# Two graph layers on one core: the second group's batches are measured together in the prologue, and its second batch takes its place among the first group's first layer

## The chip, the cores and the metric

The kernel runs on one core of one Trainium2 chip. The metric is the device time of one execution in microseconds (us); the time of record is the median of the runs shown. A profile is one further execution, taken by the hardware profiler. Engines are called as the profile calls them: PE (TensorE, matmul), PEld (its weight loads, which overlap PE), DVE (VectorE), ACT (ScalarE), POOL (GpSimd) and SP (SyncE, which issues all of this kernel's DMAs).

## The reference

The input x has 64 batches of 256 nodes with 512 features, all in float32, and one adjacency matrix of 256 by 256 serves all batches.

```python
# layer 0
h = relu(layernorm(x))
H = h @ W                                  # 512 -> 256
e = leaky_relu(H @ a[0] + (H @ a[1]).T, 0.2)
alpha = softmax(e where adj, else -1e9)
x = x + concat([alpha @ H, H])
# layer 1
h = relu(layernorm(x))
q, k, v = h @ Wq.T + bq, h @ Wk.T + bk, h @ Wv.T + bv     # 8 heads of 64
p = softmax(q k^T / 8 where adj, else -inf)
x = x + (p v) @ Wo.T + bo
```

## The kernel before, in words

**Tiling.** The 64 batches are taken in 32 groups of two. A batch is two tiles of 128 nodes (partitions) by 512 features. A group goes through first_norm (statistics, norm, a transpose into the operand hT0), first_layer (products ph with w0, attention of layer 0 with products po, then statistics, norm and transpose into hT1 for layer 1), project (q, k, v), scores, weigh and outputs. Products of layer 1 are made in seven block products instead of eight (Strassen's scheme in Winograd's form), whose operands need sums of the blocks: weight_sums and operand_sums. In the first two groups layer 0 uses plain products, four rows of ph and four of po.

**Norm and transpose.** stats gives bn_stats and bn_aggr on VectorE, factors gives minus the mean times the reciprocal deviation and that reciprocal (VectorE, then POOL), and norm gives xn on ACT, with two buffers. The first group's xn are turned on PE (pt). All others go the long way: VectorE transposes squares of 32 (xt, one buffer), SP sends them to DRAM (passed) and fetches them back in another order (moved, four DMAs), and put copies them on ACT into hT0 or hT1.

**What bounds the values.** judge checks that no score can overflow. It squares the weights on ACT, sums the squares on VectorE into `part`, and one small product on PE, `total`, adds them over the partitions. It is cut into pieces, which the driver takes through `next(verdict)`.

**The order.** Each engine works off its own queue in the order in which the program wrote it. not_sooner and after tie an instruction to the one before it on its engine, and in_order does so for every product on PE. The steps of the different groups are generators, and the driver at the end of `bounded` writes out by hand which of them takes its next step when:

- `norms` yields the pieces of first_norm of all groups, one after the other. For the second group before: measure and factors of batch 0; norm; turn and fetch; put into hT0; then the same four for batch 1.
- `pieces` yields the pieces of first_layer(1): one ph row each; with the fourth the row of scores (score_rows: a transpose on VectorE, the DMAs "line" and "own"); e and its exponential; its mask; four rows of po with their statistics, where the third also writes norm(0) and the fourth turn(0); norm(1); turn(1); put(0); put(1) with the operand sums.
- `products` yields the products of project(0), 7 each for q, k and v; `verdict` the pieces of judge; `bias` those of last_bias (bv_rows on VectorE, pb on PE); `edges` those of mask.
- late_loads issues the loads of wo_sb, bv_col, b_out and the third group's inputs on SP.

The loop over first_layer(0) (line 1068 of before) gives pieces to the numbered places of the first group's first layer. The list `order` (line 1094) then gives, for each product from the third on, first the letters n (a piece of norms) and s (a piece of first_layer(1)), and after them a piece of the verdict. After these comes the steady loop over the groups (`steps`), which the change does not touch.

Of the kernel before, what the change touches and what calls it, by code (L numbers as in the profile page):

```python
# [8 lines left out]
F32 = mybir.dt.float32  # L9
# [5 lines left out]
P = 128  # L15
# [26 lines left out]
def two_gnn_layers(tc, *args):  # L42

    nc = tc.nc
    with tc.tile_pool(name="verdict", bufs=1) as pool:
        wrong = pool.tile([1, 1], I32, name="wrong")
        bounded(tc, *args, wrong)  # L50
        again = nc.values_load(wrong[0:1, 0:1], min_val=0, max_val=1)
        with tc.If(again > 0):
            tc.strict_bb_all_engine_barrier()
            any_inputs(tc, *args)
# [3 lines left out]
def bounded(  # L58
# [27 lines left out]
    B, N, D = x.shape  # L86
    F1 = w0.shape[1]
    DH = 64
    HP = D // P
    NT = N // P  # L90
    GB = 2
# [9 lines left out]
    big = ctx.enter_context(tc.tile_pool(name="big", bufs=2))  # L101
# [81 lines left out]
    def mask():  # L183
        edge = att.tile([P, NT, N], F32, tag="kept", name="edge", bufs=3)
        not_sooner(vector, "tensor_scalar", edge, adj_i, 0.0, None, op0=ALU.not_equal)
        yield
        pt = mm("pt_mask").rearrange("p (k q) -> p k q", k=NT)
        for kb in range(NT):
            for t in range(NT):
                transpose(  # L190
                    pt[:, kb, t * P : (t + 1) * P], edge[:, t, kb * P : (kb + 1) * P], ident
                )
        not_sooner(vector, "tensor_copy", maskT, pt)

        not_sooner(vector, "reduce_max", bad[:, 0, :], edge, axis=AX.X)
        vector.tensor_scalar(bad[:, 0, :], bad[:, 0, :], 0.0, None, op0=ALU.is_equal)
        vector.tensor_tensor(edge, edge, adj_i, op=ALU.not_equal)
        vector.reduce_max(bad[:, 1, :], edge, axis=AX.X)
        yield
# [29 lines left out]
    def late_loads():  # L229
        rows = woT.rearrange("(q j h d) o -> j h d q o", j=QH, h=2, d=S)  # L230
        bv_rows = bv.rearrange("(q j h d) -> j h d q", j=QH, h=2, d=S)
        for j in range(QH):
            for half in range(2):
                not_sooner(
                    sync, "dma_start", w_sb["o"][j * S : (j + 1) * S, half, :4, :], rows[j, half]
                )
        for j in range(QH):
            for half in range(2):
                not_sooner(
                    sync, "dma_start", bv_col[j * S : (j + 1) * S, half, :], bv_rows[j, half]  # L240
                )
        not_sooner(
            sync, "dma_start", b_out,
            bass.AP(tensor=bo.tensor, offset=bo.offset, ap=[[0, P], [1, D]]),
        )
        load(2, 0)
        load(2, 1)
# [8 lines left out]
    def weight_sums(name, engine=vector):  # L256
        w = w_sb[name]
        not_sooner(engine, "tensor_sub", w[:, :, T3, :], w[:, :, W22, :], w[:, :, W12, :])
        engine.tensor_sub(w[:, :, T1, :], w[:, :, W12, :], w[:, :, W11, :])
        engine.tensor_sub(w[:, :, T2, :], w[:, :, W22, :], w[:, :, T1, :])  # L260
        engine.tensor_sub(w[:, :, T4, :], w[:, :, W21, :], w[:, :, T2, :])
# [11 lines left out]
    def last_bias():  # L273


        rows = att.tile([P, 2, D // 2], F32, tag="kept", name="bv_rows", bufs=3)
        for q in range(NQ):
            for half in range(2):
                of, by = w_sb["o"][:, half, 2 * q : 2 * q + 2, :], bv_col[:, half, q : q + 1]
                if q == half == 0:  # L280
                    not_sooner(vector, "tensor_scalar", rows, of, by, None, op0=ALU.mult)
                else:
                    vector.scalar_tensor_tensor(rows, of, by, rows, op0=ALU.mult, op1=ALU.add)
        yield
        pb = mm("pb")
        matmul(pb, square_ones, rows.rearrange("p o n -> p (o n)"), start=True, stop=True)
        yield
        not_sooner(vector, "tensor_add", b_out, pb, b_out)
        yield
# [126 lines left out]
    def stats(mv, src, t, name):  # L416
        st = small.tile([P, 6], F32, tag="st", name=f"st{name}_{t}", bufs=4)
        if vector.last:
            not_sooner(vector, "bn_stats", st, src[t])
        else:  # L420
            vector.bn_stats(st, src[t])
        vector.bn_aggr(mv[:, t, :], st)
# [87 lines left out]
    def operand_sums(engine, quads, sums):  # L510
        a11, a12, a21, a22 = quads
        s1, s2, s4 = sums
        not_sooner(engine, "tensor_add", s1, a21, a22)
        engine.tensor_sub(s2, s1, a11)

        not_sooner(engine, "tensor_sub", a21, a11, a21)
        engine.tensor_sub(s4, a12, s2)

    def seven(quads, sums):

        a11, a12, s3, a22 = quads
        s1, s2, s4 = sums
        return {
            1: (a11, W11), 2: (a12, W21), 3: (s4, W22), 4: (a22, T4),
            5: (s1, T1), 6: (s2, T2), 7: (s3, T3),
        }
# [3 lines left out]
    hT0 = {}  # L533

    def first_norm(g):

        xt = {}
        mv = small.tile([P, GT, 2], F32, tag="mv", name=f"mv0_{g}", bufs=4)
        factors, norm, turn, fetch, put = norm_T(xt, mv, f"0_{g}", g == 0)
        for b in range(GB):  # L540
            for t in range(NT):
                xt[b * NT + t] = xs[g, b][:, t, :]
                stats(mv, xt, b * NT + t, f"0_{g}")
            factors(b)
            yield
            norm(b)
            yield
            turn(b)
            if g == 1:
                fetch(b)  # L550
            yield
            if g <= 1:

                hT0[g, b] = big.tile([P, HP, N], F32, tag="hT0", name=f"hT0_{g}_{b}")
                put(b, hT0[g, b])
                if g == 1:
                    yield
        if g <= 1:
            return
        for b in range(GB):  # L560
            fetch(b, b == 1 or g == 2)
        yield
        for b in range(GB):
            hT0[g, b] = big.tile([P, HP, N], F32, tag="hT0", name=f"hT0_{g}_{b}")
            put(b, hT0[g, b])
            if b == 0:
                yield
        quads = [hT0[g, b][:, 2 * c : 2 * c + 2, :] for b in range(GB) for c in range(2)]
        sums = [
            att.tile([P, 2, N], F32, tag=tag, name=f"sums0_{g}_{tag}", bufs=bufs)  # L570
            for tag, bufs in (("r", 1), ("xn", 2), ("xn", 2))
        ]
        operand_sums(gpsimd, quads, sums)
        operands["first", g] = {i: form[0] for i, form in seven(quads, sums).items()}
        yield
# [202 lines left out]
    turn = [0]  # L778
# [279 lines left out]

    verdict = judge()
    norms = (piece for g in range(NG) for piece in first_norm(g))  # L1060
    bias, edges = last_bias(), mask()
    for piece in range(5):
# [4 lines left out]
    products, pieces = project(0), first_layer(1) if NG > 1 else iter(())  # L1067
    for piece, _ in enumerate(first_layer(0)):
        if piece == 1:
            next(norms)  # L1070
            next(norms)
            next(edges)
        elif piece == 2:
            next(norms)
        elif piece == 3:
            next(norms)
            late_loads()
        elif piece == 4 or piece == 9:
            next(verdict)
        elif piece == 10:  # L1080
            next(verdict)
            next(verdict)
            next(norms)
            next(norms)
            weight_sums("q")
        elif piece == 11:
            next(products)
            next(products)
    next(pieces)
    next(pieces)  # L1090
    next(norms)
    next(verdict)
    next(verdict)
    order = "n - - - - - nss n n ns sn ss ss s sn sn - s -".split()
    for i, parts in enumerate(order, 2):
        next(products)
        if i == 7:
# [18 lines left out]
    for g in range(NG):  # L1116
        products = project(g + 1) if g + 1 < NG else iter(())
        pieces = first_layer(g + 2) if g + 2 < NG else iter(())
# [419 lines left out]
```

## Time and profile before

| | |
|---|---|
| median of 3 runs | 2402.36 us (2402.26 to 2403.22) |
| profiled execution: its own time, its span | 2403.71 us, 2402.1 us |
| granted PE clock over the span | 0.999 |
| PE busy | 2379.1 us, 99% of the span |
| DVE, POOL, ACT busy | 1691.1, 1415.8, 1021.9 us |
| PE busy, 0 to 20 us | 10.85 us of 20 |
| PE busy, 60 to 120 us | 53.99 us of 60 |
| PE busy, 140 to 2300 us | all |

A line of a timeline reads: start, busy us, engine, line, operation, output <- input, shape, how often; in square brackets how long the engine stood before it and what released it. Nearly all lines say L35 or L137, which are those of helpers that record an instruction, so one goes by the names of the tiles. A matmul in float32 shows as two records. PEclk is the granted clock of PE as a share of full speed. A line of windows reads: the window, its length, then the busy time (and number of instructions) of PE, PEld, DVE, ACT and POOL, then PEclk, the DMA share and GB/s.

### The profile page before, as it was taken

The page shows a single profiled execution, that of the slowest core. Times are in us where ns is not written, and L with a number is a line of the kernel's source. Part 1 is how long each engine was busy: PE and PEld are TensorE (multiplying, and loading weights), DVE is VectorE, ACT ScalarE, POOL GpSimd, SP SyncE. Part 2 cuts the span into 40 slices and gives each one's busy share as a digit, 9 for nine tenths or more (in the row PEclk, how much of TensorE's full clock was granted, in tenths as well). Part 3 has the DMA queues.
Part 4 walks back from the last instruction along what each step waited for, and adds up shares of the span by engine and source line. Part 5 has one row for each costly group of instructions (what it writes and reads, how often), then busy time and mean ns, then how long its engine had stood idle before and what let it go on. Part 6 is the DMA issues. An engine that isn't in the chain of part 4 may idle for free.

```text
span 2402.1 us, 42948 instructions
## 1 busy us (share of the span) xinstructions
PE 2379.1 (99%) x15772; PEld 2005.1 (83%) x15772; DVE 1691.1 (70%) x3338; ACT 1021.9 (43%) x2017; POOL 1415.8 (59%) x1282
## 2 busy tenths in 40 slices
PE   8899999999999999999999999999999999999998
PEld 7788888888888888888888888888888888888886
DVE  7586766776766767667767677676677676676655
ACT  5543444444443434444444434344444444343431
POOL 3566556655556555666555575655665555656552
PEclk9999999999999999999999999999999999999999
DMA  6344445544454444455444555444554445444331
GB/s 197 101 137 156 134 146 154 158 145 142 136 157 149 153 151 134 144 155 157 145 141 136 159 150 159 142 136 145 154 158 146 142 136 158 150 150 152 109 105 46
DMA packets 272041, 343.76 MB, mean 143 GB/s; under 512 B 25424, under 2 KB 217168, under 8 KB 271824
## 3 DMA queue, kind: packets, MB, share of 16 engines
q1 hardware_dynamic: 271824, 340.95, 45.9%
q8 instruction: 126, 2.06, 0.4%
q14 instruction: 91, 0.75, 0.1%
HBM read 177.22 MB, written 163.64 MB: 142 GB/s over the span
## 4 chain that ended last, share of the span: by engine, by line
PE 96%; DVE 2%; DMA 1%; ACT 1%; SPq 0%; issue 0%; POOL 0%; ACTq 0%; DVEq 0%; POOLq 0%
PE pv L137 16%; PE py L137 16%; PE pk L137 16%; PE pq L137 16%; PE sc L137 10%; PE pr L137 9%; PE ph L137 8%; PE po L137 4%; DMA w_sb<-in_L_gnn_W_dram 0%; SPq L35 0%; DMA x<-in_x_dram 0%; DMA wo_sb<-in_L_gnn_Wo_dram 0%; ACT hT L35 0%; PE total L137 0%; DVE wk_sb L35 0%
## 5 line engine op out<-in xcount | busy, mean ns | idle before, releaser
L35 POOL TENSOR_TENSOR p<-p 128x512 f32<-128x512 f32 x248 | 378.7, 1539 | 491.7 <-DVE p L35 479.4
L35 ACT ACTIVATE xn<-x,factor 128x512 f32<-128x512 f32 x256 | 194.4, 807 | 329.6 <-POOL factor L35 327.7
L35 DVE TENSOR_TENSOR p<-p,maskT 128x1024 f32<-128x1024 f32 x254 | 327.6, 1309 | 3.1 <-ACT p L35 3.1
L35 DVE TENSOR_TENSOR x<-py,x 128x256 f32<-128x256 f32 x448 | 185.9, 415 | 187.4 <-PE py L137 181.0
L35 ACT ACTIVATE p<-sc 128x512 f32<-128x512 f32 x512 | 257.8, 624 | 140.9 <-PE sc L137 124.2
L35 POOL TENSOR_TENSOR parts<-parts 128x512 f32<-128x512 f32 x248 | 248.5, 1002 | 85.3 <-DMA parts<-rows 60.5
L137 PE MATMUL py<-wo_sb,oT 128*128 128x256 f32 x1024 | 262.4, 379 | 0.6 <-DVE oT L35 0.6
L137 PE MATMUL sc<-q,k 64*128 64x256 f32 x2048 | 252.3, 390 | 0.6 <-DVE oT L35 0.6
L137 PEld LDWEIGHTS sc<-q,k 64*128 64x128 f32 x2048 | 205.1, 186 | 48.4 <-issue 25.9
L137 PE MATMUL pk<-hT,wk_sb 128*128 128x256 f32 x1024 | 244.8, 382 | 0.0
L137 PE MATMUL pq<-hT,wq_sb 128*128 128x256 f32 x1024 | 240.0, 382 | 0.7 <-ACT hT L35 0.4
L137 PE MATMUL pv<-wv_sb,hT 128*128 128x256 f32 x1024 | 237.1, 379 | 0.0
L137 PE MATMUL pr<-p,v 128*32 128x256 f32 x4096 | 234.2, 380 | 0.0
L137 PEld LDWEIGHTS pq<-hT,wq_sb 128*128 128x128 f32 x1024 | 191.8, 190 | 36.2 <-issue 9.9
L137 PEld LDWEIGHTS pk<-hT,wk_sb 128*128 128x128 f32 x1024 | 189.7, 190 | 33.8 <-issue 10.4
L137 PEld LDWEIGHTS py<-wo_sb,oT 128*128 128x128 f32 x1024 | 194.2, 190 | 28.2 <-DVE oT L35 1.1
L137 PEld LDWEIGHTS pv<-wv_sb,hT 128*128 128x128 f32 x1024 | 194.4, 190 | 26.5 <-ACT kept_v L35 0.2
L35 POOL TENSOR_TENSOR factor<-factor,rexp 128x2 f32<-128x2 f32 x128 | 120.3, 940 | 162.9 <-DVE factor L35 162.7
L137 PEld LDWEIGHTS pr<-p,v 128*32 128x32 f32 x4096 | 126.8, 110 | 97.8 <-issue 17.6
L137 PE MATMUL py<-wo_sb,o_sums 128*128 128x256 f32 x768 | 197.6, 380 | 0.5 <-DVE x L35 0.5
L137 PE MATMUL pq<-sums,wq_sb 128*128 128x256 f32 x768 | 183.0, 381 | 3.4 <-ACT kept_q L35 3.4
L137 PE MATMUL pk<-sums,wk_sb 128*128 128x256 f32 x768 | 181.6, 379 | 0.5 <-ACT kept_k L35 0.5
(148 smaller groups left out, 4059.1 us busy)
## 6 DMA issues: line engine op xcount, KB each, us to landing
passed<-xt SPq DMA_DIRECT2D x124, 512.0 KB, 3.1
moved<-passed SPq DMA_DIRECT2D x496, 128.0 KB, 3.5
rows<-p SPq DMA_DIRECT2D x124, 512.0 KB, 3.4
parts<-rows SPq DMA_DIRECT2D x496, 128.0 KB, 3.0
x<-in_x_dram SPq DMA_DIRECT2D x64, 512.0 KB, 4.4
out_dram<-x SPq DMA_DIRECT2D x62, 512.0 KB, 3.9
own<-line SPq DMA_DIRECT2D x31, 256.0 KB, 3.1
wq_sb<-in_L_gnn_Wq_dram SPq DMA_DIRECT2D x2, 512.0 KB, 8.9
```

The costliest lines, as they stand in the source:

```text
L35: instruction = getattr(self.engine, operation)(*args, **kwargs)
L137: in_order(nc.tensor.matmul(*args, **kwargs))
```

## The change

For the second group, first_norm now measures both batches first, then norms, turns and fetches each in turn, and then copies both into hT0. For the other groups only the wording changes. The driver takes these pieces at other places: batch 1's measuring comes before the mask's second step, its norm and turn within the first group's first layer, and late_loads two pieces later. The second group's ph rows 0 and 1 are taken at piece 9, ahead of the first group's norm of layer 1 being turned on PE; rows 2 and 3 and the score row come ahead of the second piece of q's products that follow. In `order` the second group's attention (s) comes four to five products sooner, and the third group's norms (n) later.

```diff
@@ first_norm(g)
-        for b in range(GB):
+
+        def measure(b):
             for t in range(NT):
                 xt[b * NT + t] = xs[g, b][:, t, :]
                 stats(mv, xt, b * NT + t, f"0_{g}")
             factors(b)
+
+        def to_operand(b):
+            hT0[g, b] = big.tile([P, HP, N], F32, tag="hT0", name=f"hT0_{g}_{b}")
+            put(b, hT0[g, b])
+
+        if g == 1:
+            for b in range(GB):
+                measure(b)
+                yield
+            for b in range(GB):
+                norm(b)
+                yield
+                turn(b)
+                fetch(b)
+                yield
+            for b in range(GB):
+                to_operand(b)
+                yield
+            return
+        for b in range(GB):
+            measure(b)
             yield
             norm(b)
             yield
             turn(b)
-            if g == 1:
-                fetch(b)
-            yield
-            if g <= 1:
-
-                hT0[g, b] = big.tile([P, HP, N], F32, tag="hT0", name=f"hT0_{g}_{b}")
-                put(b, hT0[g, b])
-                if g == 1:
-                    yield
-        if g <= 1:
+            yield
+            if g == 0:
+                to_operand(b)
+        if g == 0:
             return
...
@@ driver
     for piece, _ in enumerate(first_layer(0)):
         if piece == 1:
+            for _ in range(3):
+                next(norms)
+            next(edges)
+        elif piece == 2 or piece == 3:
             next(norms)
+        elif piece == 4:
+            next(verdict)
             next(norms)
-            next(edges)
-        elif piece == 2:
-            next(norms)
-        elif piece == 3:
+        elif piece == 5:
             next(norms)
             late_loads()
-        elif piece == 4 or piece == 9:
+        elif piece == 8:
+            next(norms)
+        elif piece == 9:
             next(verdict)
+            next(pieces)
+            next(pieces)
         elif piece == 10:
             next(verdict)
             next(verdict)
-            next(norms)
-            next(norms)
             weight_sums("q")
         elif piece == 11:
             next(products)
             next(products)
+            next(norms)
     next(pieces)
     next(pieces)
-    next(norms)
     next(verdict)
     next(verdict)
-    order = "n - - - - - nss n n ns sn ss ss s sn sn - s -".split()
+    order = "- - - s - s - ss ss s sn n n n n sn - s -".split()
```

More of the change, by code (lines that the diff above doesn't have):

```diff
@@ L563, in first_norm @@
         for b in range(GB):
-            hT0[g, b] = big.tile([P, HP, N], F32, tag="hT0", name=f"hT0_{g}_{b}")
-            put(b, hT0[g, b])
+            to_operand(b)
             if b == 0:
```

## The prediction, made before the changed kernel ran

> **What bounds the kernel now.** I read the page's busy shares first, then busy time by window, then TensorE's waits, then the timeline of 20 to 135 us, where the change lies.
>
> ```profile
> PE 2379.1 (99%) x15772; PEld 2005.1 (83%) x15772; DVE 1691.1 (70%) x3338; ACT 1021.9 (43%) x2017; POOL 1415.8 (59%) x1282
> ```
>
> TensorE is the bound: 23 us of the span are not matmul. By windows, 9.2 us of that lie before 20 us (the first input), 6.6 us after 2300 us (the last output), and nothing from 140 to 2300. So the change can move only the stalls between 20 and about 135 us, and whatever TensorE loses or regains there shifts all the rest. Those stalls, by the view of waits (TensorE, 20 to 135 us: line, releaser, total, times, longest):
>
> ```profile
> PE pq L137 <- ACT kept_q L35: 3.8, 2, 3.4
> PE po L137 <- DVE e L35: 1.3, 1, 1.3
> PE sc L137 <- DVE oT L35: 0.6, 1, 0.6
> PE pk L137 <- ACT kept_k L35: 0.5, 1, 0.5
> PE pq L137 <- ACT hT L35: 0.4, 1, 0.4
> PE ph L137 <- ACT hT L35: 0.3, 1, 0.3
> ```
>
> One matters: the wait for kept_q. In the timeline of TensorE, and in two windows (busy us, then PEclk):
>
> ```profile
> 94.40 3.72 PE L137 MATMUL pq<-hT,wq_sb 128*128 128x256 f32 x16 [0.38 <-ACT hT L35]
> 101.57 3.46 PE L137 MATMUL pq<-sums,wq_sb 128*128 128x256 f32 x8 [3.45 <-ACT kept_q L35]
> 104.86 1.89 PE L137 MATMUL pq<-hT,wq_sb 128*128 128x256 f32 x8
> ...
> 108.82 1.99 PE L137 MATMUL pq<-hT,wq_sb 128*128 128x256 f32 x8 [0.34 <-ACT kept_q L35]
> ```
>
> ```profile
> 101.60:104.60 3.00, 3.00 (x7) 2.47 (x8) 3.00 (x3) 0.00 (x0) 3.00 (x2) 0.50 0.50 120
> ```
>
> TensorE stands 3.45 us, and the next product then takes 3.46 us where its like takes 1.89, at clock 0.50. The stall costs 5.0 us. The scalar queue makes it: kept_q is behind the copy of the second batch's hT, which waits 3.25 us for "moved". All stalls of 55 to 110 us together (0.3, 0.5, 1.3, 0.4, 5.0, 0.3) are 7.9 us: the most the change can win.
>
> **What the Trainium skill says.** "TensorE: Matmul & The Clock Gate", Part 1, lets the clock fall to half after an idle window of about 3.4 us; the row above agrees (3.45 us idle, then 0.50), while the 1.3 us wait left a 2.00 us product. I go by the trace: 1.57 us extra per stall over 3.4 us. "SBUF — State Buffer", section "SBUF: two separate sides", makes the port pair of VectorE and GpSimd an exclusive lock where a VectorE operation reads two SBUF inputs. The trace agrees (same operation, GpSimd first idle, then adding sums), and I price by these rows:
>
> ```profile
> 37.10 2.87 DVE L35 TENSOR_TENSOR wq_sb<-wq_sb 128x512 f32<-128x512 f32 x4
> 40.89 5.82 DVE L35 TENSOR_TENSOR wk_sb<-wk_sb 128x512 f32<-128x512 f32 x4
> ```
>
> **The change part by part**, from the built order of each queue. No work is added or removed; it is moved.
>
> (1) Batch 1's statistics go ahead of maskT. Four statistics and two factors, 2.0 us of VectorE, fall where it stood 2.08 us for pt_mask. The input was issued at about 6.3 us with 9.6 to landing, so it is there at 16. Cost 0. If that cover were gone, VectorE's 0.87 us ahead of e still hides part. On POOL its two factor operations (0.9 us) slip between residual adds whose reader, po's statistics, comes 8 us later: 0.
>
> (2) Batch 1's norm (ScalarE 26.0 to 27.5, idle before) and its two turns move ahead of the first group's second-layer statistics. On VectorE the turns take 27.3 to 28.6, so the reciprocal of po moves from 27.42 to 28.65, and with it the chain to xn.
>
> ```profile
> 32.44 1.52 ACT L35 ACTIVATE xn<-x,factor 128x512 f32<-128x512 f32 x2 [6.51 <-POOL factor L35]
> 33.40 1.27 PE L140 MATMUL pt<-ident,xn 128*128 128x128 f32 x8
> ```
>
> xn moves to 33.7 to 35.2. TensorE now wants ph of the second group's batch 0 straight after gram_k, at 33.4, and the scalar queue has that hT copy behind these two xn. Copy 35.2, first product 35.86 (0.66 after the copy's start, as at 57.80 to 58.46). **New stall S1: 2.46 us**, shorter than the clock's window, so no slow clock.
>
> (3) SyncE: passed (28.7) and four moved (31.3 to 33.1, landed by 36.5) precede wo_sb, bv_col, b_out and the third group's inputs, which slip 5.5 us. Their first users (bv_rows at 61, these statistics after 86) cover it. The row's transfer then goes line 50.8, two input loads, own 52.8; landing is 3.1 us alone, some 4.5 behind the loads: 57.3. Needed by VectorE at 59.4.
>
> (4) TensorE, start to start from before's rows: ph 3.49, pt 0.88, squares 1.79, pq 3.45, pt 0.88, ph 3.49, squares 1.78, from 35.86 to 51.6. Then five pq at 1.73; the fourth ends at 58.7. All inputs are in time: copies of hT1 at 46.4 to 47.5, POOL's sums 47.6 to 53.9. The row's transpose waits on VectorE for H (50.5), and wk_sb's sums stand behind it: at the 5.82 us of before they end at 56.6, ahead of q's sums.
>
> (5) From there VectorE is the queue that is late. After q's last sum (59.45) stand, in order: leaky e 1.49; bv_rows 0.48, 0.73, 1.41, 1.57 (before's steps, with POOL adding wo_sb between, as before); e by maskT 2.8 (0.68 each alone, about 1.65 and 1.15 against POOL's weight sums); k 0.7; wv_sb 4.24 as before; seven small sums 1.2. Sum 14.6: the first po reciprocal at 74. Two waits in between, kept_k for pk (about 1.1 us) and squares on ScalarE, stand inside this time.
>
> (6) Then the second group's second-layer statistics: three rows 1.62 apart plus 0.24 for factors, the fourth to bn_stats 1.5, a k sum 0.69, aggregate and factors 0.4: 7.6, so factor at 81.6. Now the queue order bites. ScalarE has xn of batch 1 (the "s" that calls norm(1)) **ahead of the four squares of w0**, and TensorE's "total" waits for the last sum of those squares, ahead of every pv. Before, the squares were at 73.08 and the norms came after total (75.82). Now: POOL 1.0, xn 1.56, squares 2.12, sum and semaphores 0.35: total at 86.6. TensorE, with pk and po done, is ready at 77.9. **New stall S2: 8.7 us** (part of it earlier, as pk's last product waits for that k sum). The clock falls in the first part, and one product runs before total, so I add 0.8 (0 to 1.6). What is queued behind total: seven pv 12.1 us, then scores.
>
> (7) Scores start at 86.6 + 0.25 + 12.1 + 0.8 = 99.75, against 90.10: 9.65 late. Everything feeding hT1 of group 1 is then early: its second moved lands near 95.5, the copy runs beside the scores, the kept_q stall is gone.
>
> (8) What is late next: the third group's hT copies stand ahead of the next kept_q on ScalarE. Their "moved" cannot leave before passed of its batch 1, which VectorE's turns send 5.9 us after the scores' start (95.98 before), as now. Passed and eight moved are 1.5 MB; landing was 15.1 us after the scores, about 14 without the other transfers; plus copies 1.15 and kept_q 0.9, the fourth pq starts 15.7 us after the scores, not 18.72. Of the 5.0 + 0.34 us only 3.0 come back (1.7 to 5).
>
> Sum: +9.65 - 3.0 = **+6.7 us**. Bounds: S1 2.0 to 3.0; VectorE's chain 14.6 is 10 if no port waits, 16.5 if all; later gain as said: -1 to +12. On the profiled execution (span 2402.1, own time 2403.7) that is span 2408.8, time 2410.4; on the median shown, 2402.36, it is 2409.0. About 0.2% (4.8 us) is what a measurement here can tell from no change.
>
> **Rivals.**
>
> *The port lock does not bite and VectorE keeps up (not slower).* Its place is queue step (5): where the first po reciprocal comes at 68.5 or sooner rather than 74, factor is set by po's last row from TensorE (72.7 + 3.5), total is at 81.2, scores at 93.6, 3.5 late, and 3.5 to 5 come back: -1.5 to 0, some 2401.5. For it: uncontended rows sum to 10. Against: before's bv_rows show 1.38 and 1.65 with POOL in the same place. Chance 0.24, with milder contention.
>
> *Both gifts fail (slower still).* S2 starts fully cold (1.6), own lands after 58.5, and the third group's copies stop TensorE over 3.4 us and cool it again (1.57): +11, 2413.4. Chance 0.12.
>
> *The change does what it says and no more: all stalls gone.* Then -7.9 us, 2394.5. It needs total not to wait for squares that stand behind xn; the built order excludes that unless VectorE is 8 us ahead of its rows. Chance 0.05.
>
> The likeliest, S1 and S2 with a partial return, has 0.59 and its own range 2406 to 2411.5. Slower by over 0.2% takes it and the second rival: 0.71; within 0.2% 0.24; faster 0.05. The range runs from the first rival to beyond the second: 2402 to 2414.
>
> **What would show it.** Right: TensorE waits for hT by ACT before ph at about 33.5 (2 to 2.5 us); a wait before total of several us, with PEclk near 0.5 around it, squares after four xn on ScalarE; no kept_q wait of 3.45 after the scores, but one of some 3 us ahead of the fourth pq. Wrong: total within 2 us of the last pk, VectorE idle between 60 and 80, or squares ahead of xn.

## The result, and the profile after

The changed kernel takes 2409.16 us (median of 10 runs, 2408.36 to 2410.52) against 2402.56 us for the kernel before in the same measurement (10 runs, 2402.26 to 2404.18). The ratio is 1.0026 with a 95% interval of 1.0017 to 1.0036: 6.6 us slower. The profiled execution has a span of 2408.1 us, against 2402.1.

First the page's busy times of the kernel after:

```profile
PE 2381.3 (99%) x15772; PEld 2007.2 (83%) x15772; DVE 1683.0 (70%) x3338; ACT 1021.2 (42%) x2017; POOL 1416.0 (59%) x1282
```

The numbers of instructions are the same. TensorE's busy time is 2.2 us longer, which is slow clock; the rest of the 6 us of span is standing. TensorE's waits after, 20 to 145 us (line, releaser, total, times, longest):

```profile
PE pk L137 <- DVE k L35: 3.6, 1, 3.6
PE pq L137 <- ACT kept_q L35: 3.5, 1, 3.5
PE ph L137 <- ACT hT L35: 1.4, 1, 1.4
PE total L137 <- DVE part L35: 1.4, 1, 1.4
```

Three waits that the kernel before did not have, and a wait for kept_q of the old size. The timeline of TensorE shows where each lies:

```profile
30.72 3.73 PE L137 MATMUL gram_k<-wk_sb 128*128 128x128 f32 x32
35.90 3.75 PE L137 MATMUL ph<-w_sb,hT 128*128 128x258 f32 x16 [1.45 <-ACT hT L35]
...
79.53 3.78 PE L137 MATMUL pk<-sums,wk_sb 128*128 128x256 f32 x8 [3.62 <-DVE k L35]
84.73 0.57 PE L137 MATMUL total<-part,square_ones 128*128 128x10 f32 x2 [1.42 <-DVE part L35]
85.14 5.24 PE L137 MATMUL pv<-wv_sb,hT 128*128 128x256 f32 x16
...
98.95 3.92 PE L137 MATMUL sc<-q,k 64*128 64x256 f32 x32
...
106.36 1.89 PE L137 MATMUL pq<-sums,wq_sb 128*128 128x256 f32 x8
...
115.22 3.46 PE L137 MATMUL pq<-hT,wq_sb 128*128 128x256 f32 x8 [3.52 <-ACT kept_q L35]
```

The product at 106.36 is the one that stood 3.45 us before the change; it stands no more. The one at 115.22, which stood 0.34, now stands 3.52 and runs at half clock.

One caution on reading two executions side by side. gram_k starts at 30.72 here and at 29.83 before, because the first layer's weights landed about 1 us later in this execution (VectorE waits 3.12 us for them after, 1.91 before); over the ten profiles of this study and the two of before and after that start ranges from 28.57 to 30.97 us, and the instructions ahead of the landing are the same. So I count from the start of gram_k to a later instruction of the same timeline, and take two marks: the first scores, and the first product for k behind the second batch's scores (134.66 before, 141.61 after). From that mark on TensorE is busy in both up to the tail, and what follows it takes 2266.3 to 2267.4 us in all twelve profiles.

| from gram_k's start, us | first scores | pr (p v) | second mark |
|---|---|---|---|
| before | 60.27 | 95.82 | 104.83 |
| after | 68.23 | 103.02 | 110.89 |

At the second mark the change has cost 6.06 us; the medians say 6.6. The loss to the first scores can be added up from the rows: 1.61 at ph (5.18 us behind gram_k instead of 3.57), 3.62 at pk and 1.89 because that product takes 3.78 and not 1.89, 1.42 at total, and 1.52 in the first pv (5.24 for what takes 3.72 at full clock): 10.06. The three stalls of before in this stretch (0.3, 0.5, 1.3) are gone: 10.06 - 2.1 = 7.96, which is 68.23 - 60.27. Then 1.90 us come back by the second mark.

The windows of the kernel after (length, busy time of PE, PEld, DVE, ACT and POOL, PEclk, DMA share, GB/s) show the clock low for ten microseconds, from 78.04 to 88.28:

```profile
74.63:78.04 3.41, 1.28 (x6) 0.78 (x5) 3.03 (x10) 1.10 (x2) 0.90 (x2) 1.00 0.00 0
78.04:81.46 3.42, 1.93 (x5) 1.57 (x6) 3.28 (x9) 1.03 (x2) 0.90 (x2) 0.50 0.00 0
81.46:84.87 3.41, 1.99 (x6) 1.12 (x5) 0.60 (x3) 3.32 (x12) 0.00 (x0) 0.50 0.40 158
84.87:88.28 3.41, 3.41 (x10) 2.78 (x11) 3.31 (x10) 0.25 (x1) 1.17 (x1) 0.50 0.83 271
```

And the timeline of ScalarE shows both queue orders that the forecast named:

```profile
80.85 1.52 ACT L35 ACTIVATE xn<-x,factor 128x512 f32<-128x512 f32 x2 [2.39 <-POOL factor L35]
82.28 0.40 ACT L35 ACTIVATE squares<-w_sb 128x256 f32<-128x256 f32 x1
...
111.51 1.14 ACT L35 COPY hT<-moved 128x512 f32<-128x512 f32 x2 [2.33 <-DMA moved<-passed]
113.29 1.14 ACT L35 COPY hT<-moved 128x512 f32<-128x512 f32 x2 [0.64 <-DMA moved<-passed]
114.34 0.83 ACT L35 ACTIVATE kept_q<-pq,bq_sb 128x256 f32<-128x256 f32 x2
```

The squares that total needs start only when the second batch's xn are through, and kept_q only when both copies of the third group's hT are. The larger wait, the one at pk, lies on VectorE, where the k sum stands behind the statistics of po's last row (VectorE's timeline of the kernel after):

```profile
78.80 0.67 DVE L35 TENSOR_TENSOR k<-pk,kept_k 128x512 f32<-128x512 f32 x1
```

### The profile page after: what moved, and what is told of

The parts are those of the page before. It is cut to its first block, busy times and chain, and to the rows that moved or that the text cites. A ratio compares the mean times of both kernels' runs of the same rounds, so it can differ in the third digit from the quotient of the medians.

```text
span 2408.1 us, 42959 instructions
## 1 busy us (share of the span) xinstructions
PE 2381.3 (99%) x15772; PEld 2007.2 (83%) x15772; DVE 1683.0 (70%) x3338; ACT 1021.2 (42%) x2017; POOL 1416.0 (59%) x1282
## 4 chain that ended last, share of the span: by engine, by line
PE 97%; DVE 2%; ACT 1%; DMA 0%; issue 0%; SPq 0%; POOL 0%; DVEq 0%; ACTq 0%
PE py L137 16%; PE pv L137 16%; PE pq L137 16%; PE pk L137 16%; PE sc L137 10%; PE pr L137 9%; PE ph L137 8%; PE po L137 4%; ACT xn L35 0%; DVE e L35 0%; DVE x L35 0%; DVE st L35 0%; PE pt L140 0%; DVE p L35 0%; PE total L137 0%
## 5 line engine op out<-in xcount | busy, mean ns | idle before, releaser
L35 DVE TENSOR_TENSOR p<-p,maskT 128x1024 f32<-128x1024 f32 x254 | 322.3, 1289 | 3.1 <-ACT p L35 3.1
```

The source lines that it names most:

```text
L35: instruction = getattr(self.engine, operation)(*args, **kwargs)
```

## The experiments

Ten kernels, each timed in five rounds. All but e9 start from the kernel after. The kernel before ran beside each of them, with medians of 2403.33 to 2403.60 us (2402.56 beside the kernel after), so kernels are compared by their ratios. A median carries the spread of the start told above, so the marks of the profile stand beside it.

| kernel | median us (runs) | ratio to before, 95% | first scores | second mark |
|---|---|---|---|---|
| e1_copy_first | 2407.15 (18) | 1.0018, 1.0011 to 1.0025 | 65.14 | 107.73 |
| e2_squares_first | 2409.27 (14) | 1.0024, 1.0016 to 1.0032 | 66.10 | 111.02 |
| e5_pool_later | 2406.86 (21) | 1.0016, 1.0009 to 1.0022 | 64.85 | 108.06 |
| e6_ksum_first | 2409.22 (13) | 1.0024, 1.0015 to 1.0032 | 66.92 | 111.62 |
| e4_kept_first | 2413.02 (5) | 1.0038, 1.0024 to 1.0052 | 68.54 | 113.93 |
| e9_before_kept | 2410.44 (6) | 1.0032, 1.0020 to 1.0045 | 60.39 | 112.75 |
| e7_copy_pool_squares | 2402.97 (13) | 1.0000, 0.9991 to 1.0008 | 59.13 | 103.61 |
| e8_all_four | 2405.05 (13) | 1.0007, 0.9999 to 1.0015 | 58.96 | 105.88 |
| e10_fetch_first | 2400.76 (13) | 0.9994, 0.9985 to 1.0002 | 58.94 | 103.52 |
| e12_fetch_one_put | 2404.14 (13) | 1.0004, 0.9996 to 1.0012 | 58.94 | 106.14 |

### e1: the hT copy ahead of the second batch's norm

```diff
-        elif piece == 8:
+        elif piece == 7:
             next(norms)
```

> The second group's first copy into hT0 stands ahead of the first group's two xn on ScalarE (in the changed kernel it stands behind them). Theory (queue order on ScalarE makes the stall ahead of ph): ph follows gram_k after 3.6 us instead of 5.2 and the gain runs on to the end, since VectorE's chain starts from q's fourth product: 1.3 to 1.6 us off, about 2407.7. Rival (what comes after is set by the row's transfer or by VectorE, not by q's products): the stall goes, but k's last product and total start when they did: within 0.4 us of the changed kernel.

ph follows gram_k in 3.57 us with no wait; the stall named S1 is this order on ScalarE. The second mark is 3.16 us sooner, the median 2.0 us lower (the intervals of the two ratios overlap, so it is the trace that decides). That is more than the 1.61 us of S1. The rest is clock; in the windows of this kernel it is back at 80.22 us:

```profile
76.80:80.22 3.42, 3.32 (x8) 2.52 (x8) 2.16 (x7) 1.96 (x5) 0.90 (x2) 0.50 0.28 114
80.22:83.63 3.41, 1.81 (x10) 1.42 (x9) 1.82 (x4) 2.22 (x8) 0.00 (x0) 1.00 0.43 140
```

The waits around it are as in the kernel after (3.62 and 1.60), and so is the 3.61 us product between them. Why the clock is back behind that product here, and only at 88.28 us in the kernel after, the twelve profiles show together. Between 20 and 148 us they hold 19 stretches of low clock, and these last 3.41 us (eleven), 6.83 (six) or 10.24 (two). In each of the seven profiles that have two of them, their starts lie a whole number of 3.41 us apart (78.04 and 115.58 in the kernel after: 11 times). So the clock changed only on a fixed grid of 3.41 us. Cut along this grid, the full clock fell after every step in which TensorE was busy for 1.33 us or less, and after none with 1.82 us or more. The low clock rose after every step with 2.89 us or more, and after none with 2.81 us or less. In e1 the slow product fills one step (3.32 us). In the kernel after it lies across a boundary and the wait for total follows, so two steps in a row are too empty (1.93 and 1.99 us).

So the 1.5 us hang on where the work falls on the grid. The grid's place against gram_k differs between the twelve profiles by up to 1.6 us, so a mark read in one profile holds some chance of this kind: a difference of about 1 us between two marks may be the clock's and not the edit's.

### e2: the squares ahead of the second batch's norm

```diff
+        if i == 11:
+            next(verdict)
         for part in parts:
...
-        next(verdict, None)
+        if i != 11:
+            next(verdict, None)
```

> The four squares of w0 are written before norm(1) of the second group, so that they stand on ScalarE ahead of its xn. Theory (two waits in a row: k's last product for a k sum behind po's statistics on VectorE, then total for squares behind xn): only the second goes, total follows k's last product, 1.4 us off (1 to 2), and the clock stays low. Rival (the squares behind xn are the whole loss, as the prediction's own step put first): 7 us or more off, near 2402.

total waits no more, and the scores are 2.1 us sooner than after. But nothing is left of it at the second mark. The fourth pq comes 17.46 us behind the scores, where it came 16.27 behind them after: the copies ahead of its kept_q hang on a chain of their own. Then the clock stays low for two steps of the grid (6.83 us) where after it was one, which takes another 1.07 us. The wait at pk is 3.62 us as before the edit; the one at the fourth pq reads, in TensorE's timeline of this kernel:

```profile
114.30 3.78 PE L137 MATMUL pq<-hT,wq_sb 128*128 128x256 f32 x8 [3.88 <-ACT kept_q L35]
```

The second mark is at 111.02 against 110.89, and the ratios do not tell the two apart either (1.0024 and 1.0026). Neither the 1 to 2 us of the theory nor the rival's 7 came. So the squares behind xn are a real wait of 1.42 us, and no gain shows from removing it alone: the 3.62 us at pk is due to the k sum on VectorE, not to them.

### e5: GpSimd's weight sums after the second group's chain

```diff
-        if i == 7:
+        if i == 12:
             weight_sums("o", gpsimd)
-        if i == 9:
             first_weight_sums()
```

> POOL's weight sums of wo_sb and w0 are written later, after the second group's factors, so that VectorE's bv_rows, e by mask and wv_sb sums run without POOL beside them. If the port lock makes VectorE late: its chain from leaky e to the first po reciprocal falls from 12.9 us to 8.5 to 9.5, the k sum is then ready when TensorE wants it, the clock stays full, and 3 to 5 us come off: 2404 to 2406. If only the order of the queues counts: VectorE is done sooner but waits for po's last row, and less than 1.5 us come off.

This takes GpSimd away from beside VectorE's chain. The same mask product in VectorE's timeline, first of the kernel after, then of e5:

```profile
64.33 3.43 DVE L35 TENSOR_TENSOR e<-e,maskT 128x512 f32<-128x512 f32 x2
```

```profile
62.39 1.29 DVE L35 TENSOR_TENSOR e<-e,maskT 128x512 f32<-128x512 f32 x2
```

From the leaky step to the first reciprocal of po, VectorE needs 12.90 us after (59.47 to 72.37) and 8.73 here (58.43 to 67.16): 4.2 us of the chain are GpSimd's. The wait at pk is gone, and what is left of the 5.04 us of both waits stands at total:

```profile
79.54 0.36 PE L137 MATMUL total<-part,square_ones 128*128 128x10 f32 x2 [3.20 <-DVE part L35]
```

total is 4.1 us sooner (49.88 behind gram_k, not 54.01), the second mark 2.8, the median 2.3. The 3 to 5 us expected were not reached, because this last wait again brings the clock down (the first pv take 5.39 us). Part of S2 is thus GpSimd's work beside VectorE's, as the forecast had it, and part is the order of ScalarE.

### e6: the k sum two products sooner

```diff
-    order = "- - - s - s - ss ss s sn n n n n sn - s -".split()
+    order = "- - - s - s - ss - - ssn sn sn n n sn - s -".split()
```

> Two of the four po rows are taken after k's fourth product instead of ahead of it, so that both k sums stand on VectorE ahead of these rows' statistics, and the squares ahead of xn on ScalarE. Theory (the k sum and the squares are the loss): no wait over 1 us before total, full clock, scores 5 to 7 us sooner than 98.95. Some of it goes again: kept_v now stands behind xn (up to 2 us), and the second group's hT is later, so that kept_q may stop TensorE for some us as before. Net 2 to 6 us off. Rival (the loss sits in the amount of VectorE's work, not in its order): scores no more than 2 us sooner.

Here two of po's four rows come behind k's fourth product, so that the k sums stand ahead of their statistics. Both waits, at pk and at total, are gone; total is at 47.7 instead of 54.0. So the wait at pk needs both: the k sum behind the statistics, and the long chain ahead of them (e5 removed it by the chain alone). The price appears one queue further on, again behind the second batch's xn on ScalarE (TensorE's timeline of e6):

```profile
86.12 3.78 PE L137 MATMUL pv<-wv_sb,sums 128*128 128x256 f32 x8 [3.61 <-ACT kept_v L35]
```

A stall of 3.61 us in place of one of 3.62, with the same slow product behind it. The scores come only 1.3 us sooner (the theory said 5 to 7, the rival no more than 2, though for another reason), and with 0.92 us more for POOL's sums the second mark is at 111.62: no gain. Here kept_v stands behind xn and pays in place of the squares.

### e4 and e9: kept_q ahead of the third group's copies

```diff
-                parts = "Smmnfuuumnmnuufuussssfsfssuvnfunnfsuu"
+                parts = "Smmnfuuummunnufuussssfsfssuvnfunnfsuu"
```

> In the first steps of the steady loop the two puts of the third group come one product later, so that kept_q of q's seventh form stands on ScalarE ahead of the third group's hT copies. Theory (these copies wait for moved and hold kept_q, and with it q's fourth product and the clock): that wait of 3.5 us and its half-speed product go, fourth pq 12.4 us after the scores instead of 16.3; 1 to 2 us come back as ph now reaches POOL's sums too soon. Net 3 to 4 us off, about 2405.7. Rival (the copies' data themselves are what is late, so the wait only moves to ph): under 1 us off.

> The kernel before, with only the third group's puts one product later. Theory (before, the 3.45 us wait for the second group's copy came first and gave the third group's transfers the time they need): only the 0.34 us wait goes, within 1 us of before. Rival (the kernel before is held by the same copies): 3 us off.

e9 is this edit on the kernel before. Both came out slower than any of the forecasts: the second mark is 3.0 us later than after in e4, and the median of e9 is 6.8 us above before. In e4 the wait for kept_q is gone and pr is 3.25 us sooner than after (99.77 behind gram_k). Then TensorE stops in the scores (its timeline in e4):

```profile
140.40 4.44 PE L137 MATMUL sc<-q,k 64*128 64x256 f32 x22 [4.64 <-DVE oT L35]
```

The chain is visible in two timelines of e4, SP's and VectorE's:

```profile
126.68 1.74 SPq L35 DMA_DIRECT2D parts<-rows  x4
128.45 0.54 SPq L35 DMA_DIRECT2D line<-rows  x1
132.77 0.35 SPq L35 DMA_DIRECT2D own<-line  x1
```

```profile
137.44 1.49 DVE L35 SCALAR_TENSOR_TENSOR e<-e 128x512 f32<-128x512 f32 x2 [2.66 <-ACT e L35]
138.84 0.70 DVE L35 STREAM_TRANSPOSE r<-compact 128x512 f32<-128x512 f32 x1
139.65 1.29 DVE L35 TENSOR_TENSOR oT<-pr,r 128x512 f32<-128x512 f32 x2
```

The third group's row goes line, then own, behind parts on SP; the leaky step waits for it, and r and oT, which free TensorE's scores, stand behind the leaky step on VectorE. In the kernel after the same order is there (leaky at 135.42, oT at 137.64), but pr comes later and hides it. On the kernel before the edit costs more still: e9's waits (line, releaser, total, times, longest) hold both,

```profile
PE sc L137 <- DVE oT L35: 6.1, 1, 6.1
PE pq L137 <- ACT kept_q L35: 3.4, 1, 3.4
```

because there kept_q waits for the second group's copy, which this edit does not touch. So nothing is won by removing this wait alone: behind it stands another, of 4.64 us in e4 and 6.14 in e9.

### e7: e1, e2 and e5 together

> The copy ahead of xn, POOL's weight sums later, and the squares ahead of norm(1), together; the order of q's products is left. Theory: no wait before ph, k's last product or total, scores 8 to 10 us sooner than 68.2 us after gram_k; but the kept_q wait of the third group's copies stays (3.5 to 5 us with a cold product after), so 5 to 7 us off, 2402 to 2404. Rival (the port or the queue, not both): no more than e1 and e5 give together, 4 us.

The diff is the sum of the three. The waits at ph, at pk and at total are gone; of the wait for the k sum 1.58 us are left, now at the first pv, and they do not bring the clock down. TensorE's waits in e7 (two of less than 1 us are left out):

```profile
PE pq L137 <- ACT kept_q L35: 3.9, 1, 3.9
PE pv L137 <- DVE k L35: 1.6, 1, 1.6
```

The kernel is 6.2 us faster than after and level with before, as expected. The second mark gains 7.28 us over after, more than the parts alone (3.16, 2.83 and -0.13): with only one wait removed, the next took some of it. Of the 7.28, 3.41 are the slow clock behind the two waits of S2. This shows the loss: S1 and S2, by the order of queues and by GpSimd's work beside VectorE's. It also shows what the change is worth without them. The scores are 1.14 us sooner than before, and the old kept_q stall is gone, but the wait for the third group's copies has taken its place: 3.90 us at 106.10, with a slow product.

### e8: e7 and e4's edit

> The three of the run before, and the third group's puts one product later. Theory: all stalls over 1 us between 20 and 120 us are gone but a wait of ph for POOL's sums of 1 to 2 us; 8 to 11 us off the changed kernel, 2398 to 2401, below the kernel before. Rival (a later bound in the steady loop takes the gain back, as hT of the third group or the row sums are set by DMA): not below 2402.

kept_q is free and TensorE waits 4.88 us for oT instead. The second mark is 2.3 us later than in e7. The wait behind kept_q decides here as in e4, and the rival's "not below 2402" came true.

### e10 and e12: the third group's first transfer ahead of the second's

```diff
+                if g == 2 and b == 1:
+                    fetch(0, True)
                 turn(b)
...
-        for b in range(GB):
+        for b in range(g == 2, GB):
             fetch(b, b == 1 or g == 2)
```

> The three edits of e7_copy_pool_squares (2402.97 us, equal to before), and for the third group SP issues the four moved of batch 0 ahead of passed of batch 1, instead of behind it. In e7's trace batch 0's rows have left for DRAM by about 91 us, but SP stands at passed of batch 1 until VectorE has turned it (95.4), and only then issues moved; the hT copy waits until 102.1 and kept_q behind both copies until 105.2. Theory (the order of SP's queue makes the last wait): the first hT copy starts at about 97, no wait; the second batch's moved lands some 2 us sooner, kept_q at about 103, TensorE's wait of 3.90 us falls to about 1.5 us and stays below the clock's window, so 2.5 us and 1.3 us of slow clock come back: 2399 to 2400, faster than before by 0.15%. Rival (the transfers themselves are the limit, or the rows then come late as in e4_kept_first): batch 1's moved lands when it did and the wait stays 3.5 to 4 us, or it comes back as a wait for oT: 2403 or more.

> As e10_fetch_first, and in the first steps of the steady loop one n is put one product later, so that ScalarE has kept_q between the third group's two hT copies and not behind both. Theory: kept_q does not wait for batch 1's transfer at all, TensorE's wait for it is gone, and the third group's batch 1 is late instead only where ph reads sums_xn (a wait of 0 to 1.5 us): 2397 to 2400. Rival (what e4_kept_first showed: the third group's scores row comes later on VectorE and SP, and TensorE waits 4 to 5 us for oT at clock 0.5): as much as is gained is lost again, 2402 to 2405.

e12 also has one of the two copies behind kept_q ("Smmnfuuumnmunufuu..."). In e10 the first copy no longer waits, yet kept_q comes no sooner (timeline of ScalarE in e10):

```profile
99.95 1.14 ACT L35 COPY hT<-moved 128x512 f32<-128x512 f32 x2
104.68 1.14 ACT L35 COPY hT<-moved 128x512 f32<-128x512 f32 x2 [3.59 <-DMA moved<-passed]
105.72 0.83 ACT L35 ACTIVATE kept_q<-pq,bq_sb 128x256 f32<-128x256 f32 x2
```

From passed's issue on SP (95.91) to that copy are 8.8 us, of which the issue of moved waits 2.7; TensorE's wait is 3.96 us. My theory here fell: the transfers of batch 1 set it, not what SP had ahead of them. The second mark equals e7's (103.52, 103.61), so nothing in the traces gives the edit the 2.2 us between the medians of these two measurements. e10's median is 2.7 us below before, but its interval includes no difference. e12 goes the way of e4, as its rival said: pr comes 4.1 us sooner than in e10, then the scores wait 4.50 us for oT, and the second mark is 2.6 us later. No version is shown to beat both kernels.

## Why the prediction was right, point by point

The forecast, slower and 2409.0 us, was right: S1 and S2 are the two losses, and the queues are those it named. Within S2 it set the weight wrongly. It put the stall at total, for the squares behind xn, and the k sum into a bracket. The runs show the reverse: 3.62 us stand at pk for the k sum, which VectorE reaches late, and 1.42 us at total for the squares. Counted from the end of the last pk (83.31), total follows in 1.42 us, which the forecast had listed among the signs of being wrong ("total within 2 us of the last pk"); counted from that product's start it is 5.2 us.

That the sum came so near is in part luck. The waits of S1 and S2 were put at 2.46 + 8.7 = 11.2 us and were 1.61 + 3.62 + 1.42 = 6.65; the slow clock was put at 0.8 us and was 3.41. The two errors cancel in good part.

- **(1) Statistics at no cost; (3) own.** No wait appears from the moved statistics. own was issued at 52.63 and the first step that reads it began at 57.48; the forecast said 52.8 and 57.3.
- **(2) S1.** Forecast 2.46 us, found 1.61 (5.18 - 3.57). e1 removes it by the copy's place alone. The xn before the copy started 3.1 us behind gram_k, not 3.9 as assumed.
- **(5) VectorE's chain.** Forecast 14.6 us from the last q sum, found 12.9; e5 puts the uncontended chain at 8.7 (forecast 10), so GpSimd's work beside it cost 4.2 us (forecast 4.6). The Trainium skill, "SBUF — State Buffer", section "SBUF: two separate sides", makes the port pair an exclusive lock for VectorE operations with two SBUF inputs; the mask row, 1.29 us without GpSimd and 3.43 beside it, agrees. (Beside the first of the forecast's two pricing rows GpSimd was not quite idle: its factors took 1.34 us there.) The first rival, that the lock does not bite, fell.
- **(6) S2.** Forecast total at 86.6 and 8.7 us of stall, found 84.73 (83.84 with gram_k where it was) and 3.62 + 1.42, divided as said above. From factor (79.60) to total are 5.1 us, as forecast (5.0); what was too long was the chain ahead. The term for slow clock was too small: 0.8 (0 to 1.6) against 1.89 in the last pk and 1.52 in the first pv. The page "TensorE: Matmul & The Clock Gate", Part 1, lets the full clock return after a busy window of about 3.4 us. The traces agree, if that window is read as a step of the grid shown under e1. The 3.78 us product between the two waits did not bring the clock back, because it lay across a boundary (1.93 and 1.99 us busy); the step from 84.87 to 88.28, which pv fills, did. For the same reason "shorter than the clock's window, so no slow clock", which held for S1, is no safe rule: ahead of pk the clock fell at 78.04, when TensorE had stood for 2.1 us (since 75.92), and in e5 a wait of 3.20 us was enough.
- **(7) Scores.** Forecast 9.65 us late, found 7.96, closed by the sum of rows above.
- **(8) What comes back.** Forecast 3.0 us, found 1.90, and for other reasons. The fourth pq came 16.27 us behind the scores (forecast 15.7, before 18.72), but the wait ahead of it, 3.52 us, brought the clock down again, and the product took 3.46 us at half clock, which was not costed. To pr 0.76 us came back. The other 1.14 lies between pr and the second mark, where the 0.63 us wait for oT of before is now covered and the scores beside it take 4.34 us, not 4.85; the forecast had not looked there.
- **The second rival** (both gifts fail, +11) had the cold product right and its cause: the third group's copies stop TensorE for over 3.4 us. It had own late, which it was not.

So 9.65 - 3.0 = 6.7 came true as 7.96 - 1.90 = 6.06. The two losses are shown by e1, e5 and e7, and that the larger wait hangs on the k sum by e2, e5 and e6; the sum was nearer than its terms.

## What to carry to other kernels

When work of a later group is pulled forward in hand-ordered queues, list for each engine what now stands behind it and who waits for that: here xn ahead of a copy and of four squares cost the bound engine 3 us of waiting, a sum behind statistics on VectorE 3.6, and the slow clock behind these waits 3.4 more. A wait that a change removes is worth only its distance to the next one: kept_q gave way to the next kept_q, and that to oT. So before removing a wait, walk the same stretch again with the wait gone. And cost a stall with its slow clock: in these traces, from 20 us on, every wait of 3.2 us or more brought the clock down and none of 1.6 us or less did (none lay between), at about 1.7 us for each full step of the grid in which TensorE then works.

## What the runs showed of the hardware that was not expected

- The clock of TensorE fell and rose only on a fixed grid of 3.41 us (19 low stretches of 3.41, 6.83 or 10.24 us), by how busy the step just past had been: down after 1.33 us or less, up after 2.89 us or more. The same two waits with the same product between them therefore cost ten microseconds of low clock in the kernel after and 3.42 in e1.
- gram_k's start ranges over 2.4 us (28.57 to 30.97) between profiles, over a third of what this change costs. Two things add up in it: the landing of the first weights (VectorE's first product with them starts between 9.49 and 11.26 us), and the first 16 records of ph, which take 5.31 to 6.90 us where the next 16 take 3.72, although PEclk reads 1.00 there. Marks counted from gram_k repeat better: e10 and e12, the same up to the scores, have them 58.94 us behind it both times, and the kernel after and e4, also the same up to there, 68.23 and 68.54.
